# Reordering the opening of a graph-attention kernel: two norms between products, two groups of GpSimd additions ahead of the first cycle, and one input transfer on the other queue

## The chip, the core and the metric

The kernel runs on one core of one Trainium2 chip. A core has five engines that run side by side, each with its own instruction stream in order: TensorE (PE in the profile; its weight loads are PEld), VectorE (DVE), ScalarE (ACT), GpSimd (POOL) and SyncE (SP). Transfers between the chip's main memory and the on-chip memory are started by SyncE, ScalarE or GpSimd and run on 16 shared DMA engines. The metric is the device time of one execution in microseconds (us); 1553.19 us is the median of three runs before the change (1553.01 to 1553.39).

## The reference

There are 128 batches of a matrix x with 128 rows (nodes) and 512 columns, all float32, and one 128 x 128 adjacency matrix. Two layers follow each other:

```
h = relu(layernorm(x))                      # over the 512 columns
A = adj @ h ; C = A + b                     # per batch
x = x + max over j of relu(A[:, j] + (C - A)[:, i])   # layer 0
h = relu(layernorm(x))
q, k, v = h @ Wq + bq, h @ Wk + bk, h @ Wv + bv       # 8 heads of 64
w = softmax(q k^T / 8 + mask(adj == 0))     # per head, 128 x 128
x = x + w @ v                               # layer 1
```

Layer 0 reduces to one number per row, added to all columns: max(max_j A[i, j] + b[i], 0). A constant per row does not change a layernorm that follows, but for its epsilon, so one normalised h serves both layers.

## The kernel before

**Tiling.** Batches go in groups of G = 4; there are 32 groups. For each batch, `norm` takes the mean and variance on VectorE (lines 270, 271, 273) and the power -0.5 of the variance, rstd, on GpSimd (line 275). `norm_end` subtracts the mean and clips at 0 on VectorE (line 280), multiplies by rstd on ScalarE (line 283), which gives hn, and for batches from 4 on lets GpSimd add bv to x in place (`add_bv`, line 289), since x + bv is what the output needs.

hn is used twice. `adjacency` multiplies it by the adjacency on TensorE (line 321) and takes the row maximum on VectorE (line 322). A transposed copy, HT, feeds the products with Wq, Wk and Wv. For the first four batches `transposes` makes it on TensorE; for later ones `blocks` transposes 32 x 32 blocks on VectorE (line 296) and `move` puts them in place with 16 small transfers on SyncE's queue.

**The seven products.** `Products` multiplies one group's HT by one W with the seven-product (Strassen-Winograd) scheme. p1 to p7 each are 8 TensorE matmuls (line 387) into PSUM, the memory TensorE writes, held in banks. The scheme needs four sums of quarters of the weights (`weight_sum`, line 351, tiles s1 to s4) and four of HT (`h_sum`, line 339, t1 to t4). The products run in the order p1, p6, p2, p7, p5, p4, p3. After p1, ScalarE copies the bank out twice with the bias (p1a and p1b, line 402); p2 then adds into the same bank, so it waits for both copies. p6 and then p7 share a second bank: VectorE reads it after p6 (u2, line 426) and after p7 (u3, line 435). p5 and p3 share a third bank.

**The order of work.** It is written out by hand (`manual_schedule`, line 569): each engine executes its instructions in the order in which the code emits them and waits on semaphores where data demand it. Ahead of that stand the loads: adj, x of batches 0 to 3 one by one in turn on SyncE's and ScalarE's queues (line 237), Wq on SyncE's, Wk and Wv in halves on both (line 228), then x of groups 1 and 2 on SyncE's (line 221). Biases come over GpSimd's queue.

The opening then runs: norms, transposes and adjacency of batches 0 to 3; Wv's sums on GpSimd; q of group 0 by plain matmuls in four parts (`plain_q`, each 16 matmuls and two ScalarE copies at line 465); Wk's sums and group 0's h sums on VectorE; norms and blocks of batches 4 and 5 around the third part of q; norms of 6 and 7; the fourth part; then k of group 0 with adjacency and blocks of batches 4 to 7 between its products (the table `more`, line 602).

The cycle over groups (line 611) holds, for group g: applying the weights of the group before to v, scores and exponentials of g, v of g, then q and k of g + 1. Side work is hung between the products by number (`add(s, ...)`): h sums of g + 1, masks of g, norms, blocks and adjacency of g + 2. In the first cycle alone it also holds Wq's four sums and `add_bv` of batches 0 to 3 on GpSimd.

Of the kernel before, what the change touches and what calls it, by code (L numbers as in the profile page):

```python
# [50 lines left out]
G = 4  # L51
# [113 lines left out]
def tile_adj_preln_d2(  # L165
# [13 lines left out]
    nc = tc.nc  # L179
# [22 lines left out]
    def fast(ctx):  # L202
# [9 lines left out]
        X, HN, TB, HT, HB, QT, KT, C, AMAX, WA, RSTD, MV, PR = ({} for _ in range(13))  # L212
# [13 lines left out]
        def load_w(eng, name, h):  # L226
            src = dict(q=wq, k=wk, v=wv)[name]
            eng.dma_start(
                W[name][:, 2 * h : 2 * h + 2, :],
                src[2 * h * P : (2 * h + 2) * P].rearrange("(c p) f -> p c f", p=P),  # L230
            )
# [2 lines left out]
        nc.scalar.dma_start(adj_sb, adj)  # L234
        X[0] = xpool.tile([P, G, N], F32, name="xg")
        for i in range(G):
            (nc.sync, nc.scalar)[i % 2].dma_start(X[0][:, i, :], x[i])
        load_w(nc.sync, "q", 0)
        load_w(nc.sync, "q", 1)
        nc.scalar.activation(live[:, 0:1], mhalf, AF.Copy)  # L240
# [19 lines left out]
        def norm(m):  # L260

            g, i = divmod(m, G)
            if i == 0:
                HT[g] = proj.tile([P, G, NC, D], F32, name="hT")
                AMAX[g] = stat.tile([P, G], F32, name="amax")
                C[g] = stat.tile([P, G], F32, name="c")
            HN[m] = work.tile([P, N], F32, name="hn")
            st = stat.tile([P, 6], F32, name="st")
            mv = stat.tile([P, 2], F32, name="mv")
            nc.vector.bn_stats(st, X[g][:, i, :])  # L270
            nc.vector.bn_aggr(mv, st)
            ve = stat.tile([P, 1], F32, name="ve")
            nc.vector.tensor_scalar_add(ve, mv[:, 1:2], EPS)  # L273
            rstd = RSTD[m] = stat.tile([P, 1], F32, name="rstd")
            nc.gpsimd.tensor_tensor(rstd, ve, mhalf, op=ALU.pow)  # L275
            MV[m] = mv

        def norm_end(m):
            g, i = divmod(m, G)
            nc.vector.tensor_scalar(  # L280
                HN[m], X[g][:, i, :], MV[m][:, 0:1], 0.0, op0=ALU.subtract, op1=ALU.max
            )
            nc.scalar.activation(HN[m], HN[m], AF.Copy, scale=RSTD[m])  # L283
            if m >= G:
                add_bv(m)

        def add_bv(m):
            x_m = X[m // G][:, m % G, :]
            nc.gpsimd.tensor_tensor(x_m, x_m, bv_sb, op=ALU.add)  # L289
# [21 lines left out]
        def transposes(m):  # L311
            g, i = divmod(m, G)
            ph = bank(3 + i % 2).rearrange("p (c d) -> p c d", c=NC)
            for c in range(NC):
                nc.tensor.transpose(ph[:, c], HN[m][:, c * P : (c + 1) * P], ident)
            nc.scalar.copy(HT[g][:, i], ph)

        def adjacency(m):
            g, i = divmod(m, G)
            pa = bank(5 + i % 2)  # L320
            nc.tensor.matmul(pa, adjT, HN[m], start=True, stop=True)  # L321
            nc.vector.reduce_max(AMAX[g][:, i : i + 1], pa, axis=AX.X)
            if i == G - 1:
                nc.vector.tensor_scalar(C[g], AMAX[g], b0_sb, 0.0, op0=ALU.add, op1=ALU.max)
# [16 lines left out]
        def weight_sum(eng, n, k):  # L341

            if k == 0:
                w = W[n]
                WA[n] = dict(
                    a11=w[:, 0:2, 0:HT2], a21=w[:, 0:2, HT2:N],
                    a12=w[:, 2:4, 0:HT2], a22=w[:, 2:4, HT2:N],
                    **{f"s{j + 1}": WS[n][:, j] for j in range(4)},
                )
            o, a, op, b = ("s1 a21 + a22", "s2 s1 - a11", "s3 a11 - a21", "s4 a12 - s2")[k].split()  # L350
            eng.tensor_tensor(  # L351
                WA[n][o], WA[n][a], WA[n][b], op=ALU.add if op == "+" else ALU.subtract
            )

        def weight_sums(eng, n):
            for k in range(4):
                weight_sum(eng, n, k)

        class Products:
# [47 lines left out]
            def add(self, out, bank, more):  # L407
                nc.vector.tensor_tensor(out, self.view(bank), self.view(more), op=ALU.add)  # L408
# [160 lines left out]
        with tc.manual_schedule():  # L569

            for m in range(G):
                norm(m)
                norm_end(m)
                if m in (1, 2):
                    transposes(m - 1)
            nc.vector.tensor_single_scalar(live, adjT, 0.0, op=ALU.not_equal)
            for m in (2, 3):
                adjacency(m - 2)
                transposes(m)
            adjacency(2)  # L580
            adjacency(3)
            weight_sums(nc.gpsimd, "v")
            plain_q(0, 0)
            plain_q(0, 1)
            weight_sums(nc.vector, "k")
            for k in range(4):
                h_sum(0, k)
            norm(G)
            norm_end(G)
            norm(G + 1)  # L590
            norm_end(G + 1)
            plain_q(1, 0)
            blocks(G)
            blocks(G + 1)
            move(G + 1)
            norm(G + 2)
            norm_end(G + 2)
            norm(G + 3)
            norm_end(G + 3)
            plain_q(1, 1)  # L600
            k = Products(0, "k")
            more = {
                0: [(adjacency, G)], 1: [(blocks, G + 2)],
                2: [(adjacency, G + 1), (blocks, G + 3), (move, G + 3)],
                4: [(adjacency, G + 2)], 5: [(adjacency, G + 3)],
            }
            for s, p in enumerate((k.p1, k.p6, k.p2, k.p7, k.p5, k.p4, k.p3)):
                p()
                for f, m in more.get(s, ()):
                    f(m)  # L610
            for g in range(NG):
                b = g * G
                if g > 0:
                    apply(g - 1)
                scores(g)
                v = Products(g, "v")
                if g + 1 < NG:
                    q, k = [Products(g + 1, n) for n in "qk"]
                    part = (
                        v.p1, v.p6, v.p2, v.p7, v.p5, v.p4, q.p1, v.p3, q.p6, q.p2, q.p7, q.p5,  # L620
                        q.p4, k.p1, q.p3, k.p6, k.p2, k.p7, k.p5, k.p4, k.p3,
                    )
                else:
                    part = (v.p1, v.p6, v.p2, v.p7, v.p5, v.p4, v.p3)
                todo = {s: [] for s in range(len(part))}

                def add(s, *what):
                    todo[s].append(what)

                if g + 1 < NG:  # L630
                    if g > 0:
                        for i in range(G):
                            residual(b - G + i)
                    for k in range(4):
                        add((0, 3, 5, 8)[k] if g > 0 else 4 + k, h_sum, g + 1, k)
                    if g + 2 < NG:
                        for s, l in next_norms(b + 2 * G).items():
                            for what in l:
                                add(s, *what)
                    else:  # L640
                        add(4, count, 0, b)
                    for k, s in enumerate((6, 9, 12, 13, 15, 16, 17, 18)):
                        add(s, mask, b + k // 2, k % 2)
                    if g + 3 < NG:
                        add(10, load, g + 3)
                else:
                    for k, s in enumerate((0, 0, 0, 1, 2, 2, 3, 4)):
                        add(s, mask, b + k // 2, k % 2)
                    for i, s in enumerate((0, 1, 2, 3)):
                        add(s, residual, b - G + i)  # L650
                if g == 0:
                    for s in range(4):
                        add(s, weight_sum, nc.gpsimd, "q", s)
                    for i in range(G):
                        add(8 + 2 * i, add_bv, i)
                for s, p in enumerate(part):
                    p()
                    for f, *args in todo[s]:
                        f(*args)

            g = NG - 1
            apply(g, 2)
            count(B - 2 * G, B)
            for i in range(G):
                residual(g * G + i, nc.gpsimd if i < 2 else nc.vector)
            pc = bank(1)
            for k in range(2):
                nc.tensor.matmul(pc[0:1, 0:1], CNT[k], ones, start=k == 0, stop=k == 1)
            nc.scalar.copy(flag, pc[0:1, 0:1])
# [38 lines left out]
```

## Time and profile before

| | |
|---|---|
| median time | 1553.19 us |
| span of the profiled execution | 1551.5 us |
| TensorE busy | 1530.4 us, 11805 matmuls |
| VectorE busy | 1132.9 us |
| ScalarE busy | 415.2 us |
| GpSimd busy | 274.3 us |
| mean granted TensorE clock | 0.997 |
| data moved by DMA | 105.10 MB |

"Busy" is the time in which an engine executed; what is missing to the span is waiting. A wait is put down to the instruction that ended it. The chain of work that ended last is followed back from the last instruction to what released it, step by step, so an engine's share of it says how much of the time it set. The granted clock is the share of TensorE's full clock that it was given. A table by stage gives the same busy times for stretches of the span.

Durations that recur below: a matmul group of eight at line 387 takes 1.73 us, an adjacency product 0.86 us, a row maximum 0.69 us, a GpSimd rstd 0.7 us, an `add_bv` 1.26 us, hn on ScalarE 0.72 us.

### The profile page before, as it was taken

How to read it: one execution, taken by the hardware profiler on the slowest of the kernel's cores; microseconds unless marked ns; L12 is line 12 of the kernel's file. 1: busy time of each engine (PE TensorE's matmuls, PEld its weight loads, DVE VectorE, ACT ScalarE, POOL GpSimd, SP SyncE). 2: the span in 40 equal slices, each digit the busy share in tenths (PEclk: the TensorE clock that was granted, in tenths of full speed). 3: DMA queues.
4: the chain of work that ended last, by engine and by line, in shares of the span. 5: the costliest groups of instructions: out<-in, count | busy, mean ns of one | idle time of the engine just before them, and what ended most of it. 6: DMA issues, size and time to landing. Idle time of an engine off the chain costs nothing.

```text
span 1551.5 us, 29806 instructions
## 1 busy us (share of the span) xinstructions
PE 1530.4 (99%) x11805; PEld 1311.5 (85%) x11805; DVE 1132.9 (73%) x2115; ACT 415.2 (27%) x844; POOL 274.3 (18%) x278
## 2 busy tenths in 40 slices
PE   7999999999999999999999999999999999999997
PEld 5788888888888888888888888888888888888886
DVE  7677777777777777777777777777777777777756
ACT  3222232222232222322223322223222232222221
POOL 5221221111221112211112201122111121111200
PEclk9999999999999999999999999999999999999999
DMA  5133221232322232212322222322123221232101
GB/s 181 23 79 83 55 73 49 71 82 56 79 58 61 77 83 55 73 49 72 83 55 76 53 68 79 80 57 72 49 74 83 55 75 47 72 81 67 42 30 56
DMA packets 307789, 105.10 MB, mean 68 GB/s; under 512 B 273152, under 2 KB 273280, under 8 KB 307648
## 3 DMA queue, kind: packets, MB, share of 16 engines
q1 hardware_dynamic: 306496, 101.26, 24.9%
q8 instruction: 95, 1.56, 0.4%
q10 hardware_dynamic: 976, 1.64, 0.3%
q14 instruction: 46, 0.38, 0.1%
q0 software_dynamic: 176, 0.27, 0.1%
HBM read 37.03 MB, written 33.55 MB: 45 GB/s over the span
## 4 chain that ended last, share of the span: by engine, by line
PE 96%; DVE 1%; DMA 1%; POOL 1%; issue 0%; ACT 0%; DVEq 0%; ACTq 0%; POOLq 0%
PE bk L387 74%; PE bk L512 8%; PE bk L482 8%; PE bk L321 7%; DMA wv_sb<-in_L_gnn_Wv_dram 1%; POOL sv_sb L351 0%; DVE hs L339 0%; DMA xg<-in_x_dram 0%; POOL rstd L275 0%; DVE o L530 0%; POOL xg L289 0%; DVE tb L296 0%; DVE hn L280 0%; DVE v L408 0%; ACT qT L465 0%
## 5 line engine op out<-in xcount | busy, mean ns | idle before, releaser
L275 POOL TENSOR_TENSOR rstd<-ve,mhalf 128x1 f32<-128x1 f32 x128 | 83.8, 655 | 1044.3 <-DVE ve L273 1044.3
L490 ACT ACTIVATE w<-bk 128x512 f32<-128x512 f32 x256 | 128.8, 625 | 403.4 <-PE bk L482 403.4
L289 POOL TENSOR_TENSOR xg<-xg,bv_sb 128x512 f32<-128x512 f32 x128 | 174.5, 1365 | 138.7 <-DVE hn L280 138.6
L494 DVE TENSOR_TENSOR w<-w,live 128x512 f32<-128x512 f32 x256 | 184.3, 731 | 0.6 <-ACT w L490 0.4
L387 PE MATMUL bk<-hs,sk_sb 128*128 128x256 f32 x768 | 181.1, 379 | 0.0
L387 PE MATMUL bk<-hs,sq_sb 128*128 128x256 f32 x744 | 175.7, 379 | 1.2 <-DVE u L426 0.7
L387 PE MATMUL bk<-sv_sb,hs 128*128 128x256 f32 x768 | 176.2, 379 | 0.0
L387 PEld LDWEIGHTS bk<-hs,sk_sb 128*128 128x128 f32 x768 | 145.9, 190 | 33.5 <-issue 8.1
L387 PEld LDWEIGHTS bk<-hs,sq_sb 128*128 128x128 f32 x744 | 141.2, 190 | 33.8 <-issue 9.1
L283 ACT ACTIVATE hn<-hn,rstd 128x512 f32<-128x512 f32 x128 | 92.5, 723 | 286.7 <-DVE hn L280 262.5
L387 PEld LDWEIGHTS bk<-sv_sb,hs 128*128 128x128 f32 x768 | 145.9, 190 | 19.8
L426 DVE TENSOR_TENSOR u<-bk,p1a 128x512 f32<-128x512 f32 x95 | 65.7, 691 | 127.2 <-PE bk L387 125.2
L321 PE MATMUL bk<-hn,adjT 128*128 128x512 f32 x256 | 131.4, 596 | 0.0
L512 PEld LDWEIGHTS bk<-v,w 128*64 128x64 f32 x4096 | 122.1, 137 | 10.6 <-issue 10.6
L387 PE MATMUL bk<-hT,wk_sb 128*128 128x256 f32 x512 | 122.7, 383 | 4.7 <-ACT p1b L402 4.7
L512 PE MATMUL bk<-v,w 128*64 128x65 f32 x4096 | 126.5, 222 | 0.0
L387 PE MATMUL bk<-wv_sb,hT 128*128 128x256 f32 x512 | 124.3, 386 | 0.0
L482 PE MATMUL bk<-qT,kT 64*128 64x128 f32 x2048 | 122.9, 275 | 0.0
L482 PEld LDWEIGHTS bk<-qT,kT 64*128 64x128 f32 x2048 | 116.8, 188 | 2.5 <-issue 0.3
L387 PE MATMUL bk<-hT,wq_sb 128*128 128x256 f32 x496 | 117.2, 379 | 0.0
L387 PEld LDWEIGHTS bk<-hT,wq_sb 128*128 128x128 f32 x496 | 94.2, 190 | 25.6 <-issue 14.3
L387 PEld LDWEIGHTS bk<-hT,wk_sb 128*128 128x128 f32 x512 | 98.1, 192 | 18.6 <-ACT p1b L402 5.1
(87 smaller groups left out, 1999.2 us busy)
## 6 DMA issues: line engine op xcount, KB each, us to landing
out_dram<-o SPq DMA_DIRECT2D x128, 256.0 KB, 2.1
xg<-in_x_dram SPq DMA_DIRECT2D x62, 512.0 KB, 4.3
hT<-tb SPq DMA_DIRECT2D x992, 32.0 KB, 1.9
wq_sb<-in_L_gnn_Wq_dram SPq DMA_DIRECT2D x2, 512.0 KB, 9.4
xg<-in_x_dram SPq DMA_DIRECT2D x2, 256.0 KB, 3.3
xg<-in_x_dram ACTq DMA_DIRECT2D x2, 256.0 KB, 5.8
wk_sb<-in_L_gnn_Wk_dram ACTq DMA_DIRECT2D x1, 512.0 KB, 11.2
wv_sb<-in_L_gnn_Wv_dram ACTq DMA_DIRECT2D x1, 512.0 KB, 12.4
```

The lines of the kernel that those rows point to most:

```text
L275: nc.gpsimd.tensor_tensor(rstd, ve, mhalf, op=ALU.pow)
L283: nc.scalar.activation(HN[m], HN[m], AF.Copy, scale=RSTD[m])
L289: nc.gpsimd.tensor_tensor(x_m, x_m, bv_sb, op=ALU.add)
L321: nc.tensor.matmul(pa, adjT, HN[m], start=True, stop=True)
L387: nc.tensor.matmul(bank[:, r, :], lhs, rhs, start=first and r == 0 and c == 0, stop=r == 1 and c == 1, skip_group_check=True,)
L426: nc.vector.tensor_tensor(self.u2, self.b, self.pf[0], op=ALU.add)
L482: nc.tensor.matmul(psc[j][:, f, :], KT[g][r, f, i * D : (i + 1) * D], QT[g][r, f, i * D : (i + 1) * D], start=True, stop=True,)
L490: nc.scalar.activation(w[:, j], psc[j], AF.Exp, scale=HD ** -0.5)
L494: nc.vector.tensor_tensor(w[:, j], w[:, j], live_h, op=ALU.mult)
L512: nc.tensor.matmul(pav[r, c : c + HE], w[:, h % 2, h // 2, r], V[:, i, h, :], start=True, stop=True,)
```

## The change

It touches only the opening and the first cycle, and every computation stays.

- x of batch 2 is loaded over ScalarE's queue instead of SyncE's: adj and x of 1, 2 and 3 are now on ScalarE's, x of 0 alone on SyncE's, where Wq follows at once.
- The norms of batches 6 and 7 are emitted after k's first product and second product instead of ahead of q's fourth part. The blocks of batches 6 and 7 move with them by up to one product. The aim is that ScalarE's copies of q and p1 aren't behind hn of 6 and 7.
- Wq's sums and `add_bv` of batches 0 to 3 are emitted on GpSimd right after k, ahead of the cycle, instead of between the products of the first cycle. The aim is that they aren't beside the h sums there.
- The first three h sums of group 1 are emitted one product earlier, the fourth one later (after product 8 instead of 7), in the first cycle alone.

```diff
-            (nc.sync, nc.scalar)[i % 2].dma_start(X[0][:, i, :], x[i])
+            (nc.scalar if i > 0 else nc.sync).dma_start(X[0][:, i, :], x[i])
...
             move(G + 1)
-            norm(G + 2)
-            norm_end(G + 2)
-            norm(G + 3)
-            norm_end(G + 3)
             plain_q(1, 1)
             k = Products(0, "k")
             more = {
-                0: [(adjacency, G)], 1: [(blocks, G + 2)],
-                2: [(adjacency, G + 1), (blocks, G + 3), (move, G + 3)],
+                0: [(adjacency, G), (norm, G + 2), (norm_end, G + 2)],
+                1: [(norm, G + 3), (norm_end, G + 3), (blocks, G + 2)],
+                2: [(adjacency, G + 1)], 3: [(blocks, G + 3), (move, G + 3)],
                 4: [(adjacency, G + 2)], 5: [(adjacency, G + 3)],
             }
...
+            weight_sums(nc.gpsimd, "q")
+            for m in range(G):
+                add_bv(m)
             for g in range(NG):
...
-                        add((0, 3, 5, 8)[k] if g > 0 else 4 + k, h_sum, g + 1, k)
+                        add((0, 3, 5, 8)[k] if g > 0 or k == 3 else 3 + k, h_sum, g + 1, k)
...
-                if g == 0:
-                    for s in range(4):
-                        add(s, weight_sum, nc.gpsimd, "q", s)
-                    for i in range(G):
-                        add(8 + 2 * i, add_bv, i)
```

## Prediction

> **What bounds the kernel now.** I read the engine totals first, then a table of busy time by stage, then who waited for whom on TensorE, then the chain of work that ended last, from 24 to 55 us. The totals say where any gain must be:
>
> ```profile
> PE 1530.4 (99%) x11805; PEld 1311.5 (85%) x11805; DVE 1132.9 (73%) x2115; ACT 415.2 (27%) x844; POOL 274.3 (18%) x278
> ```
>
> TensorE is busy for 1530.4 of 1551.5 us, so 21.1 us are all that an order of work can win. The table by stage (length, then busy time and count of PE, PEld, DVE, ACT, POOL, the granted clock, the DMA share, GB/s) places them:
>
> ```profile
> 0.00:20.00 20.00, 13.36 (x51) 9.20 (x52) 12.58 (x28) 7.37 (x13) 9.04 (x18) 1.00 0.89 314
> 20.00:40.00 20.00, 15.35 (x64) 12.59 (x63) 14.88 (x25) 6.64 (x14) 13.10 (x12) 0.94 0.17 39
> 60.00:80.00 20.00, 18.83 (x83) 15.25 (x82) 17.69 (x28) 4.73 (x10) 12.20 (x11) 1.00 0.09 15
> 1500.00:1552.00 52.00, 42.90 (x467) 38.18 (x466) 30.64 (x60) 9.63 (x21) 2.48 (x2) 0.94 0.11 42
> ```
>
> TensorE's idle time is 6.64 us in the first stage, 4.65 in the second, 1.17 in the third, and 8.6 at the end (51.5 - 1500 - 42.90), which nothing in this change touches. From 80 to 1500 us it is never idle: whatever moves TensorE's stream early moves the end by as much. The waits of TensorE up to 90 us:
>
> ```profile
> PE bk L256 <- POOL ident masks.py:199: 4.7, 1, 4.7
> PE bk L387 <- ACT p1b L402: 4.7, 1, 4.7
> PE bk L315 <- ACT hn L283: 1.9, 3, 1.3
> PE bk L387 <- DVE u L426: 0.7, 1, 0.7
> PE bk L387 <- DVE hs L339: 0.5, 1, 0.5
> ```
>
> The second line is the 4.65 us: p2 of batch group 0's k adds into the bank of p1 and must wait until ScalarE has copied p1 out twice (p1a, p1b). The last two are the 1.17 us. The chain shows why p1b is late:
>
> ```profile
> 31.77 0.65 POOL rstd L275
> 32.42 0.66 POOL xg L289
> ...
> 33.61 0.74 POOL rstd L275
> ...
> 34.37 0.03 ACT hn L283
> ...
> 35.00 0.82 ACT qT L465 x2
> 35.82 0.73 ACT p1a L402 x2
> 36.55 0.74 ACT p1b L402 x2
> 37.29 0.04 issue
> 37.33 3.61 PE bk L387 x8
> ```
>
> The products were ready long before: p1 ended at 29.93 by the timeline. But ScalarE's next instructions were the norms of batches 6 and 7 (hn at L283), which waited for GpSimd's rstd. The last line holds a second loss: the 8 matmuls of p2 took 3.61 us, the same 8 later take 1.73. The granted clock read 0.50 from 38 to 40 us.
>
> **What the Trainium skill says.** *TensorE: Matmul & The Clock Gate*, Part 1: a TensorE left idle for a window of about 3.4 us runs at half clock until a busy window has passed. The trace agrees: 4.65 us idle, then the 3.61 us above, a loss of 1.88. The same page, "Architectural detail": ScalarE's queue is strictly first in, first out. It agrees: qT, p1a and p1b sat ready behind hn. *SBUF — State Buffer*, "Who interferes with whom": a VectorE instruction with two SBUF inputs blocks against a GpSimd one that reads SBUF. It agrees: the h sums (hs, L339) take 1.75 us while GpSimd adds weights and 0.68 after. *DMA: Bandwidth & Descriptors*, "Queues, rings and completion order": each DMA engine serves the rows of SP and ACT in turn, each row in its own order. So a transfer's place in its row matters, which the next lines (KB each, median us to landing) bear out:
>
> ```profile
> xg<-in_x_dram SPq DMA_DIRECT2D x2, 256.0 KB, 3.3
> xg<-in_x_dram ACTq DMA_DIRECT2D x2, 256.0 KB, 5.8
> ```
>
> SP's two are x0 and x2 (3.0 and 3.6 us), ACT's are x1 and x3: 3.8 and, third behind adj and x1, 7.8.
>
> **Part 1, norms 6 and 7 after p1.** Removed from ScalarE ahead of p1a: two waits for rstd and two hn. Worked from the trace's own times: hn of batch 5 ends at 29.82, then qT of plain_q(1,0) 0.72 to 30.55, qT of plain_q(1,1) (TensorE done at 28.2) 0.72 to 31.3, p1a 0.73 to 32.0, p1b 0.74 to 32.8. TensorE meanwhile does p1 to 29.93, adjacency(4) 0.86 to 30.79, p6 1.73 to 32.52. p2 could start at 32.84 instead of 37.33, at full clock: it ends at 34.57 instead of 40.94, **6.37 us** earlier.
>
> What queues behind the moved norms? VectorE: amax(4) at 30.8, statistics of 6 (0.6+0.19+0.17) and its hn (0.48) to 33.0, u2 (waits p6) to 33.6; p7, which writes u2's bank, is due only after p2 and adjacency(5), 34.57+0.86 = 35.4. Norm 7 and the transpose of 6 take VectorE to 35.7, amax(5) to 36.4, free when p7 ends (37.2). GpSimd: rstd 6 at 32.65, add_bv(6) 1.26, rstd 7 to 35.35. ScalarE: hn 6 to 34.1, hn 7 to 36.1, then p2's kT, whose bank is next written in the scores, at 44. adjacency(6) and (7) need them near 39 and 41.5. All slack: cost nothing.
>
> **Part 2, Wq's sums and bv at once on GpSimd.** Same eight instructions, moved. They run from about 36.6 to 47 us (4 sums of 1.26 to 1.7, 4 adds of 1.26), where GpSimd was idle from 36.8 to 59.8 by the timeline. VectorE then does work with one SBUF input (adds from banks, maxima, a transpose), so nothing is blocked. In the first cycle, the h sums no longer meet them (1.53, 1.38 and 1.75 us return to 0.68) and start one product earlier; t2 is ready some 3.5 us before q.p6 wants it. The two waits go: **1.17 us**.
>
> **Part 3, x2 on ACT's queue.** This is no gift. x2 takes the place of x3 (landed at 1.65+7.8 = 9.45) and x3 comes after it. How long 256 KB more take in ACT's row: what was left on that queue from 8 us on and from 10 us on was
>
> ```profile
> q10 hardware_dynamic: 533, 1.02, 19.0%
> ...
> q10 hardware_dynamic: 414, 0.78, 15.1%
> ```
>
> that is 0.24 MB in 2 us, so 2.2 us for 0.262 MB; from 6 to 8 us it was 1.30 to 1.02 MB, 1.9 us. With full halves of the 390 GB/s seen after 11 us it would be 1.3. I take 2.0: x3 at 11.45. Before, x3's statistics began at 9.47 and plain_q on TensorE at 14.39, through hn, transposes(3) and the last adjacency products; all of that chain moves by 2.0, plain_q to 16.4. Other end: TensorE reached transposes(2) only at 10.37, so if DMA had no pause (there is one from about 4.6 to 5.6 us, 21 GB/s at its lowest) x3 might land as before: 0.
>
> What is lost is less than 2.0, because Part 1 leaves TensorE waiting 0.32 us for p1b. plain_q ends at 30.2, p1 at 31.9, adjacency(4) 32.8, p6 34.5. VectorE's Wk sums began at 16.0, waiting for Wk; now they begin after c at 15.55+2.0 = 17.55, a shift of 1.55, so p1b ends near 34.35, in time. p2 runs 34.5 to 36.25: 4.69 us earlier than before instead of 6.37. Wk and Wv land when the same bytes have moved; GpSimd's Wv sums stay near 17.4.
>
> **Sum.** 4.69 + 1.17 = 5.86 us: 1553.19 - 5.86 = **1547.3**.
>
> **Rivals.**
> 1. *x3 is not late* (for: the pause may fall elsewhere, and SP sends less ahead of Wk; against: the third place in ACT's row took 7.8 us). 6.37 + 1.17 = 7.54: 1545.7.
> 2. *Late x, and a second cold clock.* With x2 near 9.4, TensorE has nothing from about 10.4 to 12.2. For: the clock fell after 4.65 idle us. Against: this gap is 1.8, and the clock held through a 3.4 us window that was idle for about 1.5 us (30.7 to 34.1, 1.95 busy). Cost 1.88: 1549.2.
> 3. *The waits come back*: VectorE or GpSimd is behind with norms 6 and 7, and p7, adjacency(6) or the h sums wait as p2 did. For: GpSimd's rstd sits behind adds of 1.26 us. Against: the slack above. Half the gain back, with late x: 1550.2, near no change.
> 4. *Slower*: x3 lands as late as Wk's half on the same queue did (2.23+11.2 = 13.4, 4.0 later instead of 2.0), a cold clock comes with it (1.88), and ScalarE's wait of 4.65 reappears in k's products: 1547.3+2.0+1.9+4.65 = 1555.9. It needs three failures at once.
>
> **How the numbers follow.** Forecast 57%, rival 1 22%, rival 2 10%, rival 3 7%, rival 4 4%. 1545.3 to 1549.5 holds the first three with the bounds of the x delay (1.3 to 2.2); about 11% lie outside above. Faster by over 3.1 us (0.2%) means under 1550.1: the first three and a little of rival 3, 0.90; the rest of rival 3, and half of rival 4, whose 2.7 us over is under the bound, within, 0.08; slower 0.02.
>
> **What would show it.** Part 1: no wait of TensorE for p1b over 0.5 us, p2's 8 matmuls in 1.73 us, no half clock after 30 us. Part 2: GpSimd's four sq sums in one run before 48 us, h sums of group 1 at 0.7 us, no TensorE wait between 60 and 80. Part 3: VectorE's waits for xg grow from 4.3 us (2.88 for x0, 1.41 for x3) to about 6.4 (2.9 for x2, 0.6 for x3), and plain_q starts at about 16.4. The prediction is wrong if x3 lands under 10 or over 12.5, if the clock falls early, or if TensorE waits on VectorE among k's products.

## The result, and the profile after

The changed kernel takes 1546.79 us (median of 6 runs, 1545.5 to 1547.62); the kernel before took 1553.63 (median of 6 runs, among them the three given at the start). The ratio is 0.9953, with a 95% interval from 0.9941 to 0.9966: 6.8 us faster, where 5.9 were forecast. A second series gave 1547.93 against 1553.97, ratio 0.9957 (0.9943 to 0.9971), 6.0 us.

The totals of the page after:

```profile
PE 1528.1 (99%) x11805; PEld 1310.5 (85%) x11805; DVE 1129.9 (73%) x2115; ACT 415.2 (27%) x844; POOL 272.4 (18%) x278
```

The span is 1544.7 us, so TensorE is idle for 16.6 us instead of 21.1. It is also busy for 2.3 us less with the same 11805 matmuls. Most of that is clock, not work: the profile of before has 3.41 us at half clock after the wait for p1b, worth 1.7 us, and the profile after has no half clock there. The table by stage, with the columns as before:

```profile
0.00:20.00 20.00, 12.12 (x45) 7.97 (x46) 11.85 (x26) 7.12 (x13) 9.97 (x19) 1.00 0.91 326
20.00:40.00 20.00, 20.00 (x91) 16.85 (x90) 16.84 (x31) 7.63 (x17) 12.26 (x12) 1.00 0.13 26
60.00:80.00 20.00, 20.00 (x91) 16.85 (x90) 16.77 (x30) 5.73 (x13) 5.27 (x5) 1.00 0.31 67
1500.00:1552.00 52.00, 36.01 (x436) 32.12 (x434) 27.32 (x54) 8.86 (x19) 2.49 (x2) 0.94 0.11 42
```

The stages from 20 to 40 and from 60 to 80 us are now full; the first lost 1.24 us more than before. TensorE's waits up to 90 us are two, both in the first 14 us:

```profile
PE bk L256 <- POOL ident masks.py:199: 4.7, 1, 4.7
PE bk L315 <- ACT hn L283: 3.1, 3, 2.4
```

The waits for p1b, u and hs are gone, and the wait for hn grew from 1.9 to 3.1. The chain that ended last, from its start to 36 us:

```profile
2.19 8.62 DMA xg<-in_x_dram
...
10.84 0.71 DVE st L270
...
12.02 0.73 POOL rstd L275
...
12.77 0.73 ACT hn L283
...
13.55 0.65 PE bk L315 x4
14.20 1.72 PE bk L321 x4
15.92 13.81 PE bk L458 x64
29.73 1.73 PE bk L387 x8
31.46 0.86 PE bk L321 x2
32.32 3.45 PE bk L387 x16
```

This is most of the change in one view. Before, the chain ran over Wv's transfer, GpSimd, VectorE and ScalarE to p1b at 37.3 us. Now it is TensorE alone from q's first product on, and p6 and p2 are one block of 16 matmuls in 3.45 us. But what starts TensorE is now the last x, issued fourth on ScalarE's queue, behind adj, x1 and x2. Two narrow views of the issues, of x1 and of x3 (KB, us to landing):

```profile
xg<-in_x_dram ACTq DMA_DIRECT2D x1, 256.0 KB, 5.1
```

```profile
xg<-in_x_dram ACTq DMA_DIRECT2D x1, 256.0 KB, 8.6
```

x1, issued at 1.20, landed at 6.3 instead of 5.0; x3, issued at 2.19, at 10.8 instead of 9.45. q's first product begins 1.4 us later than before.

GpSimd's moved additions, by its timeline after (start, duration):

```profile
38.12 1.27 POOL L351 TENSOR_TENSOR sq_sb<-wq_sb 128x512 f32<-128x512 f32 x1
...
41.92 1.27 POOL L351 TENSOR_TENSOR sq_sb<-wq_sb,sq_sb 128x512 f32<-128x512 f32 x1
43.14 4.97 POOL L289 TENSOR_TENSOR xg<-xg,bv_sb 128x512 f32<-128x512 f32 x4
```

They run back to back and are over at 48.1; VectorE's first h sum of group 1 begins only at 56.8.

### The profile page after: what moved, and what is told of

Same layout as the page of the kernel before. It is cut to its first block, busy times and chain, and to the rows that moved or that the text cites. A ratio compares the mean times of both kernels' runs of the same rounds, so it can differ in the third digit from the quotient of the medians.

```text
span 1544.7 us, 29809 instructions
## 1 busy us (share of the span) xinstructions
PE 1528.1 (99%) x11805; PEld 1310.5 (85%) x11805; DVE 1129.9 (73%) x2115; ACT 415.2 (27%) x844; POOL 272.4 (18%) x278
## 3 DMA queue, kind: packets, MB, share of 16 engines
q8 instruction: 95, 1.56, 0.4%
## 4 chain that ended last, share of the span: by engine, by line
PE 98%; DMA 1%; DVE 0%; ACTq 0%; ACT 0%; POOL 0%; DVEq 0%; issue 0%
PE bk L387 75%; PE bk L512 8%; PE bk L482 8%; PE bk L321 7%; PE bk L458 1%; DMA xg<-in_x_dram 1%; DVE o L530 0%; ACTq L237 0%; DVE o L540 0%; DVE live L552 0%; ACT hn L283 0%; POOL rstd L275 0%; DVE st L270 0%; PE bk L315 0%; DVE RS L529 0%; DVEq L668 0%
## 5 line engine op out<-in xcount | busy, mean ns | idle before, releaser
L387 PE MATMUL bk<-hs,sk_sb 128*128 128x256 f32 x768 | 181.1, 379 | 0.0
L387 PE MATMUL bk<-sv_sb,hs 128*128 128x256 f32 x768 | 176.2, 379 | 0.0
L387 PE MATMUL bk<-hs,sq_sb 128*128 128x256 f32 x744 | 175.6, 379 | 0.0
L387 PEld LDWEIGHTS bk<-hs,sk_sb 128*128 128x128 f32 x768 | 145.9, 190 | 33.5 <-issue 7.9
L387 PEld LDWEIGHTS bk<-hs,sq_sb 128*128 128x128 f32 x744 | 141.4, 190 | 32.0 <-issue 7.2
L387 PEld LDWEIGHTS bk<-sv_sb,hs 128*128 128x128 f32 x768 | 145.9, 190 | 19.8
L387 PE MATMUL bk<-wv_sb,hT 128*128 128x256 f32 x512 | 124.3, 386 | 0.0
L387 PE MATMUL bk<-hT,wk_sb 128*128 128x256 f32 x512 | 121.0, 379 | 0.0
L387 PE MATMUL bk<-hT,wq_sb 128*128 128x256 f32 x496 | 117.2, 379 | 0.0
L387 PEld LDWEIGHTS bk<-hT,wq_sb 128*128 128x128 f32 x496 | 94.2, 190 | 25.6 <-issue 14.3
L387 PEld LDWEIGHTS bk<-hT,wk_sb 128*128 128x128 f32 x512 | 97.3, 190 | 13.2
```

The lines of the kernel that those rows point to most:

```text
L387: nc.tensor.matmul(bank[:, r, :], lhs, rhs, start=first and r == 0 and c == 0, stop=r == 1 and c == 1, skip_group_check=True,)
```

## The experiments

My theory: the gain is TensorE's idle time and its half clock, taken out by the norms (part 1) and by the GpSimd additions (part 2); the transfer (part 3) costs. The rival: the transfer pays for itself, since Wv's sums begin 0.95 us sooner on GpSimd in the changed kernel (16.46 against 17.41 by its timelines). The times below are set against the kernel before in the same series (medians 1554.19, 1554.11 and 1553.97).

**The norms alone.** The kernel before, with only this:

```diff
-            norm(G + 2)
-            norm_end(G + 2)
-            norm(G + 3)
-            norm_end(G + 3)
             plain_q(1, 1)
...
-                0: [(adjacency, G)], 1: [(blocks, G + 2)],
-                2: [(adjacency, G + 1), (blocks, G + 3), (move, G + 3)],
+                0: [(adjacency, G), (norm, G + 2), (norm_end, G + 2)],
+                1: [(norm, G + 3), (norm_end, G + 3), (blocks, G + 2)],
+                2: [(adjacency, G + 1)], 3: [(blocks, G + 3), (move, G + 3)],
```

> Only the norms of batches 6 and 7 move behind k's first products; x of batch 2 stays on SyncE's queue and GpSimd's sums stay in the first cycle. Theory (TensorE's idle time and its half clock are the whole gain): the wait for p1b falls from 4.65 to about 0.3 us, p2's eight matmuls take 1.73 instead of 3.61 us, the two waits of 1.17 us stay: 6.2 to 6.4 us faster than before, about 1547.2. Rival (the gain of the changed kernel came from Wv landing 0.95 us sooner over the other queue, or from the GpSimd sums): under 4 us faster, above 1549.5. What I add over the prediction: in this kernel the first of Wq's sums still follows norm 7 on GpSimd, so nothing new is in the way of p2.

Measured: 1547.08 us, ratio 0.9954 (0.9941 to 0.9968), 7.1 us faster. TensorE's waits after the first batches are just the two of the first cycle:

```profile
PE bk L387 <- DVE u L426: 0.7, 1, 0.7
PE bk L387 <- DVE hs L339: 0.5, 1, 0.5
```

Part 1 alone gives as much as the whole change. The transfer isn't needed for the gain. From profile to profile it gives a little less: the span falls from 1551.5 to 1545.1 us, by 6.4.

**The GpSimd additions alone.** The kernel before, with `weight_sums(nc.gpsimd, "q")` and the four `add_bv` ahead of the cycle, and the h sums one product earlier.

> Only Wq's sums, bv's four additions and the h sums of the first cycle move. Theory: the wait of 4.65 us and the half clock stay, the waits of 0.45 and 0.72 us in the first cycle go: 1.2 us faster than before, about 1552.3. Rival (the waits come from VectorE's own load, not from GpSimd beside it): no change within 0.4 us, with the waits still there, or moved to another product.

Measured: 1552.28 us, ratio 0.9989 (0.9983 to 0.9996), 1.9 us faster with an interval from 0.6 to 2.6. The waits for u and hs are gone from its profile. The theory's 1.2 us lies inside; the rival's no change doesn't. How much the two waits cost can be read from the first score product of group 0 (q k^T, line 482) and the last small copy of the program (the flag), first in the kernel before, then here:

```profile
50.42 3.84 PE L482 MATMUL bk<-qT,kT 64*128 64x128 f32 x64
1545.14 0.15 ACT L669 CAST flag<-bk 1x1 int32<-1x1 f32 x1 [11.49 <-PE bk L668]
```

```profile
51.92 3.84 PE L482 MATMUL bk<-qT,kT 64*128 64x128 f32 x64
1545.00 0.15 ACT L667 CAST flag<-bk 1x1 int32<-1x1 f32 x1 [11.49 <-PE bk L666]
```

That is 1494.72 us before and 1493.08 here, 1.64 less. The norms alone and the transfer alone leave the stretch as it was (1494.71 and 1494.72), and the changed kernel has 1493.08 too. The profile shows something else, in the table by stage:

```profile
36.00:38.00 2.00, 0.00 (x0) 0.00 (x0) 0.74 (x2) 1.96 (x6) 1.92 (x3) 0.57 0.31 52
38.00:40.00 2.00, 1.99 (x5) 1.63 (x6) 0.57 (x1) 0.00 (x0) 2.00 (x3) 0.50 0.31 53
40.00:42.00 2.00, 2.00 (x6) 1.56 (x5) 0.00 (x0) 0.17 (x1) 2.00 (x3) 0.50 0.31 52
42.00:44.00 2.00, 2.00 (x6) 1.05 (x5) 0.59 (x1) 0.67 (x2) 2.00 (x3) 0.72 0.12 20
```

After a wait for p1b of 4.8 us, as long as before, the clock (the seventh number) stays at half from 36.3 to 43.1 us, twice as long as in the profile of before. Part of that falls into the wait: from p2's start to the first score product it takes 13.9 us here, 13.1 in the profile of before and 11.4 where the clock did not fall (the next run), so the half clock cost 2.5 us here and 1.7 before.

**The transfer alone.** The kernel before, with x of batches 1, 2 and 3 on ScalarE's queue.

> Only x of batch 2 moves to ScalarE's queue. Theory: x1, x2 and x3 land late (near 6.3, 8.7 and 10.8 us as in the changed kernel), q's first matmul starts near 15.8 instead of 14.4, and as the chain over VectorE and GpSimd that ends in p1b begins behind the adjacency maxima it shifts too, but by less, since Wv lands 0.95 us sooner and h sums meet fewer GpSimd operations: 0.5 to 1.2 us slower than before, about 1554.3. Rival (the transfer helps: Wv sooner moves the whole chain to p1b): 0.5 us or more faster than before. Clock: p2 stays at half clock.

Measured: 1554.74 us, ratio 1.0005 (0.9997 to 1.0014): 0.55 us slower by the medians, but not parted from no change. The rival's 0.5 us faster lies outside the interval. In its profile q begins at 16.5 and p1b is waited for 3.7 us instead of 4.7: p2 begins 1.2 us later than before while q begins 2.1 later, so the chain to p1b isn't held up by the late x as much as q is. I expected p2 at half clock; in this profile it isn't:

```profile
38.00:40.00 2.00, 1.46 (x7) 1.31 (x8) 1.10 (x2) 0.48 (x2) 0.00 (x0) 1.00 0.30 50
```

That execution was the fastest of its 13 (1552.86). So the half clock after the wait comes in some executions and not in others. The mean granted clock of each execution says the same: it is 0.998 in this profile, 0.997 in the one of before (3.4 us at half after the wait) and 0.996 in the one of the additions alone (6.8 us). Of the 13 executions here, three read 0.998 (1552.86 to 1554.42 us), five 0.997 (1554.52 to 1554.76) and five 0.996 (1555.34 to 1556.39). Of the 75 executions of the kernel before in the three series, 58 read 0.996, 16 read 0.997 and one 0.998. If the last digit is read this way, nearly all of them lost the clock, and most lost more of it than the profile of before shows; the norms alone have 0.998 or 0.999 in all five.

**The changed kernel without the transfer,** twice; the second time beside the changed kernel on one chip.

```diff
-            (nc.scalar if i > 0 else nc.sync).dma_start(X[0][:, i, :], x[i])
+            (nc.sync, nc.scalar)[i % 2].dma_start(X[0][:, i, :], x[i])
```

> The changed kernel with x of batch 2 back on SyncE's queue. Theory: q starts at 14.4 again, 1.37 us earlier than in the changed kernel, and TensorE then waits some 0.3 us for p1b: 0.8 to 1.1 us faster than the changed kernel, about 1545.8, 7.5 us faster than before. Rival (the transfer pays for itself by freeing the chain to p1b): p1b is later than in the changed kernel by more than TensorE gains, and the time is that of the changed kernel, 1546.8, or above.

> The changed kernel as it is, beside the one without its transfer on the same chip. Both theories: 1546.8, 0.9953 of before.

> The changed kernel with x of batch 2 back on SyncE's queue, a second time, on the same chip as the changed kernel. Theory (the transfer only delays x1 and x3): 0.8 to 1.1 us faster than the changed kernel. Rival (the difference seen was between two chips or two days): within 0.4 us of it.

Measured: 1545.71 us (ratio 0.9945, 0.9931 to 0.9959) and 1545.90 (0.9946, 0.9933 to 0.9960), against 1547.93 for the changed kernel beside the second. It is faster by 2.0 us on the same chip, 1545.65 to 1546.16 against 1547.13 to 1548.48 with no overlap: the rival falls, and the cost is above the 0.8 to 1.1 that I expected. Why, shows in this second profile of the changed kernel (the slowest of its five runs, 1548.48), TensorE's timeline:

```profile
12.16 1.12 PE L315 MATMUL bk<-ident,hn 128*128 128x128 f32 x4 [0.83 <-ACT hn L283]
13.07 1.92 PE L321 MATMUL bk<-hn,adjT 128*128 128x512 f32 x2
15.04 1.12 PE L315 MATMUL bk<-ident,hn 128*128 128x128 f32 x4
...
17.83 13.98 PE L458 MATMUL bk<-hT,wq_sb 128*128 128x256 f32 x64
```

The chain that ended last in this profile says what q waited for:

```profile
2.19 10.12 DMA xg<-in_x_dram
...
14.27 0.73 ACT hn L283
...
15.04 1.12 PE bk L315 x4
```

x3 landed at 12.3 instead of 10.8, and over its norm and hn it still sets the start of the last transposes, at 15.04 instead of 13.55. TensorE was also still at half clock: transposes take 1.12 us a batch, where the first profile of the changed kernel shows 0.60 at 11.66 already, and full clock came only at 16.3 us by the trace's record. From the last transposes to q it takes 2.8 us instead of 2.2. So of the 2.1 us by which q begins later than in the first profile (17.8, not 15.8), about 1.5 are the late x3 and 0.6 the clock.

**Filling the wait.** The kernel before, with matmuls into an unused bank between p6 and p2. First nine, then five:

```diff
-                0: [(adjacency, G)], 1: [(blocks, G + 2)],
+                0: [(adjacency, G)], 1: [(blocks, G + 2), (filler, 9)],
```

> The kernel before with nine matmuls into an unused bank between p6 and p2 (their result is never read), so that TensorE is busy while it waits for p1b; nothing else moves. It parts the wait of 4.65 us from the half clock that follows. Theory (the clock falls because TensorE was idle, and how often depends on where its clock windows lie): p2 starts at the same time, 37.3 us, but its eight matmuls take 1.73 us in every run; the mean gain is what the half clock cost on average, 1 to 2 us, about 1552.3 beside runs of the kernel before of 1554.2, with less spread. Rival (the half clock has nothing to do with being idle, or p2's first matmuls are slow for another reason): no change within 0.4 us, p2 still 3.6 us.

> The kernel before with five matmuls (0.86 us each, 4.3 us together) into an unused bank between p6 and p2 (their result is never read) instead of nine, whose 7.7 us reached 2.9 us past p1b's end. Theory (half clock from idle time): TensorE is busy from p6 to some 0.5 us ahead of p1b, p2 starts with p1b near 37.1 us and takes 1.73 us in every run; the time is that of nine fillers less 2.9 us, about 1551.9, 2.2 us faster than before; that is what the half clock cost on average. Rival: p2 is slow for another reason; no change within 0.4 us.

Nine took 1554.77 us, ratio 1.0004 (0.9996 to 1.0013): the expected gain did not come. I had taken 0.43 us for a filler, half of what it takes. The timeline of TensorE:

```profile
32.23 7.89 PE L453 MATMUL bk<-wq_sb,adjT 128*128 128x512 f32 x18
39.96 1.89 PE L387 MATMUL bk<-hT,wk_sb 128*128 128x256 f32 x8
```

The fillers ended 2.9 us after p1b, which was done at 37.05. p2 did run at full clock, so the gain was there and was spent. Five fillers took 1552.05 us, ratio 0.9987 (0.9981 to 0.9994), 1.9 us faster, with

```profile
33.06 4.46 PE L453 MATMUL bk<-wq_sb,adjT 128*128 128x512 f32 x10
37.78 1.99 PE L387 MATMUL bk<-hT,wk_sb 128*128 128x256 f32 x8 [0.26 <-ACT p1b L402]
```

p2 starts as late as before and takes 1.8 us. So the half clock comes from the idle time, and costs 1.9 us on average (0.9 to 3.0), apart from the wait itself. All 34 executions with fillers, nine or five, have a mean granted clock of 0.998 or 0.999; the 42 of the kernel before beside them have 0.996 or 0.997. The 21 runs with five span 1551.45 to 1553.13; the kernel before spans 1552.93 to 1555.84 beside them, so the clock is part of that kernel's spread.

**What is left in the opening.** All on top of the changed kernel without the transfer. Norms of batches 4 and 5 ahead of the last two h sums of group 0:

```diff
-            for k in range(4):
+            for k in range(2):
                 h_sum(0, k)
             norm(G)
...
             norm_end(G + 1)
+            for k in (2, 3):
+                h_sum(0, k)
```

> The kernel with the norms moved and x of batch 2 back on SyncE's queue, and with the norms of batches 4 and 5 ahead of the third and fourth h sums of group 0 on VectorE. Theory: p1b waits on the chain from norm 4 over rstd, hn and the copies of q; norm 4 starts some 2.4 us earlier, p1b is done before p6 ends, TensorE's last wait of 0.5 us in the opening goes: 0.5 us faster than without this, about 1545.2. Rival (the copies of q and p1 are themselves the limit, or the late h sums hold p7): no gain, or TensorE waits for hs at p7 instead.

1545.6 us (0.9945, 0.9932 to 0.9959): no gain that can be told from 1545.71. The wait for p1b, 0.5 us in the profile without this, is gone, but it is absent too in the second profile without this, where q began at 15.0 instead of 13.7. What the reordering frees, the opening's own variation covers.

x3 on SyncE's queue, Wq's second half on ScalarE's:

```diff
-            (nc.sync, nc.scalar)[i % 2].dma_start(X[0][:, i, :], x[i])
+            (nc.scalar if i == 1 else nc.sync).dma_start(X[0][:, i, :], x[i])
         load_w(nc.sync, "q", 0)
-        load_w(nc.sync, "q", 1)
+        load_w(nc.scalar, "q", 1)
```

> The kernel with the norms moved, with x0, x2 and x3 on SyncE's queue ahead of Wq's first half and only x1 and Wq's second half on ScalarE's. Theory (what counts is how many bytes stand ahead of a transfer in its own row, and the rows share the engines evenly): x3 lands near 7.5 to 8 us instead of 8.7 to 9.5, all four batches by 8; TensorE's cold products then set q's start at 13.7 us at the earliest, and the chain over Wk and p1b is as it was: 0 to 0.4 us faster than with x2 back alone, about 1545.5. Rival (Wq or Wk becomes the wait, since Wq's second half shares ScalarE's queue with x1): TensorE waits for Wq before q's first product, or x1 lands later than 5.0: slower by 0.5 us or more.

1545.19 us (0.9944, 0.9931 to 0.9958), 0.5 us under 1545.71, about what was expected, though the ranges overlap (1544.51 to 1545.6). The last x landed by 7.3 us (issued at 1.65, at most 5.6 to landing), and VectorE waited for x once, for x0. TensorE did not wait for Wq. But the gain isn't seen in the opening: q begins at 14.71 and the first score product at 44.13, where the two profiles without this have 43.88 and 44.45. It shows at the very end, where the last output transfer lands in 3.1 us, and in 3.9 in both of those. From the last small copy (flag) to the end of the span it is 5.5 us here and 5.4 in the run with everything together below, and 6.3 to 6.5 in all other profiles. Whether the new order of the loads has to do with that, no run shows.

Eight matmuls on a constant tile ahead of the first transpose, alone and with both of these:

```diff
+        pw = bank(7)
+        for k in range(6):
+            nc.tensor.matmul(pw[:, 0:256], warm[:, 0:P], warm, start=True, stop=True)
         pt = bank(0)
         nc.tensor.transpose(pt[:, :D], adj_sb, ident)
+        for k in range(2):
+            nc.tensor.matmul(pw[:, 0:256], warm[:, 0:P], warm, start=True, stop=True)
```

> As the run before, with eight matmuls on a constant tile ahead of the transpose of adj (their result is never read) and nothing else. Theory (with x2 back, the chain from Wk over norm 4 to p1b sets when p2 starts, so q earlier brings nothing): q starts 0.7 to 1.2 us earlier, TensorE waits that much longer for p1b, the time changes by less than 0.3 us. Rival (TensorE's own opening is the limit and all of the 1.8 us gained with everything together came from the clock): 0.8 us or more faster.

> Both of these together, and eight matmuls on a constant tile ahead of the transpose of adj (their result is never read), to bring TensorE to full clock before its first products. Theory: with a clock near full from about 8 us on, adjacency(0) takes 0.86 instead of 1.75 us, q starts near 13.0 instead of 13.7 to 14.4, p1b is in time, and the whole stream follows: 1.0 to 1.5 us faster than with x2 back alone, about 1544.4. Rival (the clock falls again in the gaps between the first products, or Wq, landing near 13, becomes the wait): no more than the gain of the norms of 4 and 5, 0.5 us.

Alone: 1545.46 us (0.9945, 0.9932 to 0.9959), 0.4 under the 1545.90 beside it, with overlapping ranges. q began at 13.7, at full clock, and the gain turned into a wait (lines are seven later in this file: L394 is L387, L409 is L402):

```profile
PE bk L394 <- ACT p1b L409: 1.2, 1, 1.2
```

Together: 1543.89 us, ratio 0.9935 (0.9922 to 0.9949), the fastest of all, 1.8 us under the version without the transfer in the series before. By the profiles (spans of 1541.2 and 1543.3 us) 1.2 of 2.1 us are gained up to the first score product (42.71 instead of 43.88) and 0.9 at the very end, where the last output transfer again lands sooner (2.9 us). TensorE's timeline:

```profile
8.56 1.02 PE L328 MATMUL bk<-hn,adjT 128*128 128x512 f32 x2
...
13.28 13.98 PE L465 MATMUL bk<-hT,wq_sb 128*128 128x256 f32 x64
...
31.41 1.89 PE L394 MATMUL bk<-hT,wk_sb 128*128 128x256 f32 x8
```

adjacency(0) is at full clock (1.02 by the timeline, 1.56 to 1.92 in the profiles without), and p2 begins at 31.4, with no wait for p1b. None of the three alone moves p2 forward like this: it begins at 32.52 with the norms, 32.83 with x3 and 33.22 with the eight matmuls, against 32.48 and 33.15 without any. TensorE's opening and the chain to p1b are nearly level, which fits that both have to move; pairs of the three were not run.

## Why the prediction was right

The forecast, 1547.3, lies between the two medians, 1546.79 and 1547.93, and the gain came by the mechanism that was named. In the first profile of the changed kernel the first score product comes 5.24 us earlier than before (45.18 instead of 50.42), where 4.69 were forecast, and the stretch behind it is 1.64 shorter, where 1.17 were forecast: 6.88 us. That the forecast is so close to both medians is in part luck. The late x alone moves q by 2.1 us between two profiles of the same kernel; in the second the first score product comes only 3.2 us earlier than before (47.26).

- **Part 1.** p2 without wait and at full clock, as forecast. 6.37 us were worked out for x on time; alone it gave 6.4 from profile to profile and 7.1 by the medians. The difference fits the clock: the profile that the sum was worked from lost 3.4 us to half clock, and most executions of the kernel before read as having lost more. The 1.88 for it was one execution's, and a little high: a p2 that starts after a wait at full clock takes 1.8 us, not 1.73, and by the starts of the products the loss was 1.7. The filled wait puts the mean at 1.9; single profiles show none (the transfer alone) and 2.5 (the GpSimd additions alone). The slack claimed for what queues behind the moved norms held: no wait of TensorE among k's products.
- **Part 2.** 1.17 forecast, 1.9 measured with an interval that holds it, and 1.64 by the profiles. The forecast took the idle time alone, but q.p6 and q.p7 begin 0.61 and 0.87 us later than a product each 1.73 us would put them (68.73 and 73.99), and each then takes 0.07 to 0.08 longer. The h sums did not all return to 0.68: the third took 1.25 in the changed kernel, where `add_bv` of batch 9 stands beside it on GpSimd at 59.66. No wait followed: q.p7, which uses it, comes five products later.
- **Part 3.** Forecast as a cost, and it is one. x3 was put at 11.45 and q at 16.4; the two profiles show 10.8 and 12.3, 15.8 and 17.8. What the working missed: x1 too comes later (6.3 and 5.8 in the two profiles instead of 5.0), with Wq next to it on SyncE's queue where x2 was. So VectorE's waits for x are 2.9, 1.0, 0.9 and 0.6 us for x0 to x3, 5.5 in all, and not 6.4 with 2.9 of them for x2. Why x1 loses anything, when transfers stood on SyncE's queue beside it before as well, stays open: no run parts it. The net cost at the end, 1.68 by the sum (6.37 less 4.69), measured 2.0 on one chip and 1.1 across two series. By the first score product it is 1.3 in one pair of profiles (45.18 against 43.88) and 2.8 in the other (47.26 against 44.45).
- **Rival 2,** the second cold clock, was set beside the forecast at 10%. No profile of the changed kernel shows the clock fall in the opening, but one of the two shows it rise late, at 16.3 us instead of 11.6. That cost q 0.6 us, where 1.88 were put. How often it comes, two profiles can't tell.
- **Rivals 1, 3 and 4** did not come. Rival 1's time, 1545.7, is that of the kernel with x on time: 1545.71 and 1545.90.
- **A slip.** The idle time at the end of the kernel is printed as 51.5 - 1500 - 42.90; it is 1551.5 - 1500 - 42.90, and the 8.6 us are right.

## What to carry to other kernels

On an engine that works strictly in order, look at what stands ahead of the instruction that frees the bottleneck: two norms whose results TensorE takes in only after k's fifth and sixth products held two copies that its third product, p2, was waiting for. A bundle of edits should be taken apart even when it wins: one of the three here gave back 1.1 to 2.0 of the 8.5 us that the other two gain together (1554.19 to 1545.71). Where two chains are nearly level, as TensorE's opening and the way to p1b are here, shortening either alone brings next to nothing.

## What the runs showed of the hardware that was not expected

- The same wait of 3.7 to 4.8 us on TensorE was followed by full clock in one profile, by 3.4 us at half in another, and by 6.8 us in a third. The traces' records of the granted clock fit windows of 3.41 us that lie differently in each execution, as the Trainium skill has it (*TensorE: Matmul & The Clock Gate*, Part 1): before, it changes at 10.24, 37.55 and 40.96 us; with the GpSimd additions alone at 12.40, 36.29 and 43.12, each distance a multiple of 3.41. Laid on TensorE's timelines, the windows that lost the clock were busy for 0.2 us (before) and 0.4 us (additions alone); those that the wait touched in the transfer's profile were busy for 1.6 and 1.5 us, and kept it. A share that kept the clock did not bring it back: with the additions alone, the window from 36.29 to 39.70 was busy for 1.7 us, and the clock stayed at half through the next. That the share of a window decides is an inference from these few. Five matmuls of no use, about 0.9 us each, in that wait made the kernel 1.9 us faster.
- TensorE came to full clock at 11.6 us in one profile of the changed kernel and at 16.3 in another, which had a gap of 0.83 us between its first adjacency product and the next transposes; with eight matmuls of no use, of which the first began at 1.24 us, it came before 6.5 us (the transpose of adj took 0.27 instead of 0.47).
- The last output transfer of 256 KB took 3.9 to 4.1 us to land in the profiles where it was read, but 3.1 and 2.9 in the two with Wq's second half on ScalarE's queue, and the span behind the last small copy is 0.9 us shorter there. No run here shows why.
- A wait cost TensorE more than the idle time that the profile gives for it: two waits of 0.45 and 0.72 us lengthened the stream by 1.64.
- DMA slowed at 4.5 to 5.5 us of the kernel before, to 21 GB/s in one half microsecond, with x of batch 3 (issued at 1.65, landed at 9.45) still on its way. In the changed kernel it slowed at 5 to 6 us, to 144 and 148 GB/s. No run here shows why.
